# Cross attention in a perceiver layer on one core: scores computed once, their maxima reduced through 32 by 32 turns, elementwise work moved from VectorE

## The chip, the core and the metric

The kernel runs on one NeuronCore of a Trainium2 chip. TensorE (PE) multiplies matrices into PSUM, VectorE (DVE), ScalarE (ACT) and GpSimd (POOL) do the rest, SyncE (SP) issues transfers. The metric is the device time of one execution in microseconds (us), the median of several runs; lower is better. The profile is of one execution, and its spans and waits come from that one.

## The reference, cut to what matters

64 batch elements have 64 tokens of 256 features each, and each element has its own context of 256 tokens. One layer has three residual steps:

```python
x = x + xattn(layernorm(x), ctx, ctx)   # 16 heads of 16 features, keys and values from ctx
x = x + attn(layernorm(x))              # causal self attention, 16 heads
x = x + ffn(layernorm(x))               # silu(gate) * up, then down; inner width 1024
...
q = (queries @ Wq.T + bq).reshape(B, L, H, E)
k = (keys @ Wk.T + bk).reshape(B, S, H, E)
scores = jnp.einsum('blhe,bshe->bhls', q, k)
attn = jax.nn.softmax(scores * scale, axis=-1)
out = jnp.einsum('bhls,bshe->blhe', attn, v).reshape(B, L, H * E)
return out @ Wo.T + bo
```

In the FFN, activations are rounded to 8-bit integers with one scale per row (127 over the row's largest magnitude) and weights to -1, 0, 1 with one scale per matrix, ahead of each of the three products.

## The kernel before, in words

The elements are taken in nine groups (`GB`): seven of 8 and two of 4. Three stages of three groups run at the same time: cross attention of group g, self attention of group g-1, FFN of group g-2. Nothing is a loop over stages in program order. `layers` describes every step as an operation with an engine, an estimated cost, a due time `at` (one unit is about one batch element), and the buffers it reads and writes. `Graph.run` then plans: at each step it takes, over the engines, the operation that can start first, choosing on one engine by due time, by how much later it could start (`LATE`), and by whether ScalarE would have to load another function table (`TURN`); `AHEAD` bounds how far it may run in front of the oldest one left. `SHIFT` and `LAST` are per-kind offsets of the due times, `LAST` for those due after `END`, and `HURRY` and `SPURT` draw the last elements forward. The plan fixes the order on each engine; on the chip each engine goes through its list strictly in that order. Buffers come from rings with a few slots (`RINGS`). The score ring `sc` has one slot, [128, 4, 2, 256] f32, which is four of the eight PSUM banks; the other four banks are the ring `mm`, through which all other products pass.

Per pair of elements, `project` makes keys (line 484, evicted at 507) and values (519, evicted at 525). Per element, `cross` (line 587) does this:

1. `sc`, line 607: scores with queries on the partitions (two heads times 64 tokens), keys along the row, 4 head pairs at a time in four row groups of TensorE, twice.
2. `nm`, line 620: DVE takes the negated maximum of each row, 2048 elements to 8. `sc`'s slot is then free.
3. `terms`, lines 613 to 616: four small DVE steps split each maximum into three bf16 terms.
4. `mtp` (625) turns them on TensorE, and ACT copies them to `mT` (627).
5. `scT`: in the same kind of slot, the scores a second time, now with keys on the partitions. Line 638 first writes minus the maximum through a selecting matrix `sel` (bf16), line 643 adds the scores.
6. `exp`, line 648: two ACT steps of 1024 elements into `PT`, which frees the slot.
7. `av`, line 656: products with the values. The value tile carries ones, so that the same product gives the sums. Two heads share a product, and each half of the partitions has its numerators where the other has its sums.
8. `keep` (ACT, 672) scales one half by a 0/1 column, DVE merges it with the other half (677), shuffles the sums (678), takes their reciprocal (679), and POOL multiplies into `yT` (682).

Self attention uses the same `sc` slot for its scores `ssc` (line 725), twice per group; its hold ends when four mask additions on DVE (737) have read it. In the FFN, ACT normalises (459), DVE finds the row maxima (819) and multiplies each tile by its scale, adding a number that rounds (862); 512 columns at a time TensorE makes gate and up (882), ACT applies silu (889), and DVE multiplies up, its scale and silu (892) into `h`. Then come the row maximum, the rounding (ACT 908, DVE 911), a turn by transfer, and the product down (919).

`out_bias` (line 369) makes the two output bias rows once, near the start, from constants `brow` that were loaded over ACT's queue (1016).

Of the kernel before, what the change touches and what calls it, by code (L numbers as in the profile page):

```python
# [48 lines left out]
SC = S // P  # L50
GB = (8, 8, 8, 8, 8, 8, 8, 4, 4)
# [44 lines left out]
class Op:  # L96
# [15 lines left out]
STICK = 0.0005  # L112
TABLE = 1283.0
AHEAD = 5.691
HURRY, SPURT = 2.4886, 8
WAIT = 578031
LATE = 0.0129
TURN = 2.8858
# [6 lines left out]
    "ACT exp": -0.11, "ACT hqT f": -10.14, "ACT hscaled f": 1.99, "ACT k s": 0.18, "ACT keep": -0.9,  # L125
    "ACT mT": 1.22, "ACT norm a": 0.11, "ACT norm f": -2.03, "ACT norm s": 2.98, "ACT q s": -0.85,
    "ACT qT f": -11.74, "ACT sexp s": -0.59, "ACT silu f": -0.43, "ACT skeep s": 1.07, "ACT spT s": -3.21,
    "ACT turned a": -1.44, "ACT v a": -2.48, "ACT v s": -0.49, "DVE h f": 0.9, "DVE hq f": 0.13,
    "DVE hscales f": 1.37, "DVE mask s": 0.027, "DVE nm": 0.73, "DVE q f": 2.75, "DVE ratio": 0.51,
    "DVE rounded f": 3, "DVE smax s": 0.07, "DVE stats a": -2.45, "DVE stats f": -3.39, "DVE stot s": 0.805,  # L130
    "DVE wdown sums": 1.47, "DVE x a": -1.84, "DVE x f": 1.05, "DVE x s": 1.31, "PE av": -0.29,
    "PE down f": -0.64, "PE gate/up f": 0.1, "PE k a": 0.05, "PE mtp": 0.12, "PE q a": -0.24,
    "PE q s": 0.03, "PE sav s": -1.58, "PE sc": -0.38, "PE ssc": -0.13, "PE stp s": 0.21,
    "PE turn a": -0.11, "PE turn s": -1.7, "PE v a": -0.1, "PE v s": 2.11, "PE wgate total": 0.98,
    "POOL less s": -1.59, "POOL root a": 2.36, "SP load wgate": 1.56, "SP load wup": 1.17,
    "SP load x": -6.63,
# [3 lines left out]
    "ACT exp": -2.03, "ACT hqT f": 9.14, "ACT hscaled f": 1.51, "ACT keep": -0.53, "ACT mT": -2.79,  # L140
    "ACT norm s": -5.27, "ACT qT f": 9.17, "ACT sexp s": -1.13, "ACT silu f": 1.38, "ACT spT s": 2.36,
    "ACT v a": 3.26, "ACT v s": 1.58, "DVE h f": -0.28, "DVE hq f": 1.39, "DVE hscales f": 1.92,
    "DVE mask s": -1.27, "DVE nm": -2.37, "DVE q f": -2.35, "DVE ratio": 1.17, "DVE rounded f": -1.88,
    "DVE smax s": 0.59, "DVE stats f": 1.64, "DVE stats s": 2.35, "DVE stot s": -0.66, "DVE syT s": -0.92,
    "DVE x f": 2.71, "DVE x s": -2.93, "PE down f": 3.91, "PE gate/up f": 0.21, "PE hqtp f": 2.44,
    "PE k a": 3.27, "PE mtp": 1.86, "PE o s": -2.39, "PE sc": -0.79, "PE ssc": -1.18, "PE stp s": -0.27,
    "PE v a": -1.05, "PE v s": -1.66, "POOL less s": 2.66,
}
END = 59.061
# [177 lines left out]
def dve(n):  # L327
    return 65.0 + 1.044 * n
# [6 lines left out]
def layers(nc, a, out, R, c):  # L335
# [9 lines left out]
    msl = [Buf(t=c[f"msl_{i}"]) for i in range(2)]  # L345
# [23 lines left out]
    def out_bias(at, w, vcol, brow, res, name):  # L369

        rep = bufs("keep", [P, KC, P], f"rep_{name}")
# [4 lines left out]
        def product():  # L376
# [5 lines left out]
        op("DVE", dve(D), at, name, lambda: nc.vector.tensor_tensor(res.t, pm.t[:, 0:D], brow, ALU.add),  # L382
           reads=[pm], writes=[res])
# [203 lines left out]
    def cross(n, at):  # L587
# [5 lines left out]
        nm = bufs("nm", [P, NJ, KC], f"nm_{n}")  # L593
        ms = msl[n % 2]

# [6 lines left out]
        sc = bufs("sc", [P, NJ, KC, S], f"sc_{n}")  # L602

        def maxima():
            for hg in range(KC):
                for j in range(NJ):
                    nc.tensor.matmul(sc.t[:, j, hg, :], q(hg, j), kT.t[rows(j), hg, k0:k0 + S],  # L607
                                     start=True, stop=True)
# [373 lines left out]
def tile_perceiver(ctx: ExitStack, tc: tile.TileContext, a: dict, out: bass.AP):  # L982
# [32 lines left out]
    for i, name in enumerate(("bo_r", "bo2_r")):  # L1015
        nc.scalar.dma_start(c["brow"][:, i, :], a[name])
# [103 lines left out]
```

## Time and profile before

| | |
|---|---|
| median of 3 runs | 861.35 us (861.09 to 861.81) |
| profiled execution: its own time / its span | 862.48 us / 860.7 us |
| granted TensorE clock, mean | 0.99 |
| busy: PE / weight loads / DVE / ACT / POOL | 831.4 / 573.2 / 690.3 / 590.4 / 301.0 us |
| function table loads on ACT | 44 of 1.28 us |
| transfers | 41.8 MB, mean 49 GB/s |

The span is what the instructions cover in the profiled execution; that execution's own time is 1.8 us longer. Busy times are sums over an engine's instructions. In a group's row, the name of the written tile stands left of `<-` and those of the read ones right of it, then partitions x elements and type, then the count; after the first bar the busy time and the mean of one instruction, after the second the engine's idle time before them and what ended it. An f32 product appears as two matmul instructions. In the page's list of costliest groups the first two are the maxima over the scores (DVE, 144.7 us) and the exps (ACT, 125.1 us); the products of keys and of values follow with 122.7 and 122.6 us.

### The profile page before, as it was taken

The numbers are of one execution on the slowest core, as the hardware profiler recorded it, in microseconds if no ns is written. First come the engines' busy times: TensorE is split into PE (matmuls) and PEld (weight loads), VectorE is DVE, ScalarE is ACT, GpSimd is POOL, SyncE is SP. The second block draws the span as 40 slices with busy tenths as digits, with TensorE's granted clock in tenths as the row PEclk, the third lists the DMA queues.
The fourth block names the chain that finished last, engine by engine and source line by source line (L and its number), as shares of the span: only waits on it lengthen the run. The fifth ranks groups of instructions, "written<-read, shape, count | busy, mean of one in ns | idle before, by whom it ended". The sixth has DMA issues, their size and how long they took to land. (4 is left out here: it accounts for less than half of the span.)

```text
span 860.7 us, 28167 instructions
## 1 busy us (share of the span) xinstructions
PE 831.4 (97%) x12136; PEld 573.2 (67%) x12136; DVE 690.3 (80%) x1499; ACT 590.4 (69%) x948; POOL 301.0 (35%) x505
## 2 busy tenths in 40 slices
PE   8999899999999999999999999999999999998966
PEld 5766657776577756676667766777567775776633
DVE  2587678896888878988789886889779877999995
ACT  3554666547986597747886487865888487767855
POOL 3330527424242334405144152422344141354640
PEclk9999999999999999999999999999999999999988
DMA  7212201002022210222112111211012320011110
GB/s 264 76 51 100 75 27 51 27 3 62 14 51 64 57 40 6 51 88 39 38 38 51 39 39 39 50 58 51 8 39 51 64 38 14 14 27 39 26 37 38
DMA packets 47740, 41.82 MB, mean 49 GB/s; under 512 B 39168, under 2 KB 39680, under 8 KB 47616
## 3 DMA queue, kind: packets, MB, share of 16 engines
q1 hardware_dynamic: 45888, 39.59, 17.5%
q8 instruction: 95, 1.56, 0.7%
q10 hardware_dynamic: 1728, 0.43, 0.2%
q14 instruction: 29, 0.24, 0.1%
HBM read 26.65 MB, written 4.19 MB: 36 GB/s over the span
## 5 line engine op out<-in xcount | busy, mean ns | idle before, releaser
L620 DVE TENSOR_REDUCE nm<-sc 128x8 f32<-128x2048 f32 x64 | 144.7, 2261 | 27.9 <-PE sc L607 27.9
L648 ACT ACTIVATE PT<-scT 128x1024 f32<-128x1024 f32 x128 | 125.1, 1020 | 28.4 <-PE scT L643 28.1
L484 PE MATMUL k_a<-cT,wk 128*128 128x512 f32 x256 | 122.7, 609 | 2.5 <-DMA wk<-in_wk_dram 2.5
L519 PE MATMUL v_a<-wv,cT 128*128 128x256 f32 x512 | 122.6, 383 | 0.0
L682 POOL TENSOR_TENSOR yT_a<-keep 128x128 f32<-128x128 f32 x64 | 30.7, 480 | 247.7 <-DVE keep L679 189.0
L519 PEld LDWEIGHTS v_a<-wv,cT 128*128 128x128 f32 x512 | 95.0, 190 | 19.6 <-issue 3.2
L742 POOL TENSOR_TENSOR s_s<-s_s,smax_s 128x512 f32<-128x512 f32 (+1 forms) x72 | 67.3, 951 | 60.5 <-DVE smax_s L740 56.8
L507 ACT ACTIVATE kT<-k_a,bk_c 128x512 f32<-128x512 f32 x64 | 43.9, 685 | 59.4 <-PE k_a L484 59.1
L656 PEld LDWEIGHTS av<-PT,v 128*32 128x32 f32 x4096 | 60.4, 110 | 28.6 <-ACT PT L648 13.0
L484 PEld LDWEIGHTS k_a<-cT,wk 128*128 128x128 f32 x256 | 46.4, 192 | 47.5 <-issue 39.0
L752 POOL TENSOR_TENSOR s_s<-s_s,stot_s 128x512 f32<-128x512 f32 (+1 forms) x72 | 67.1, 952 | 27.6 <-DVE msl L613 12.3
L607 PE MATMUL sc<-kT,qm 32*128 32x256 f32 x1024 | 73.3, 400 | 3.0 <-ACT PT L648 3.0
L643 PE MATMUL scT<-qm,kT 32*128 32x128 f32 x2048 | 75.1, 270 | 0.0
L677 DVE SCALAR_TENSOR_TENSOR keep<-av,par,keep 128x256 f32<-128x256 f32 x64 | 30.6, 479 | 53.6 <-ACT keep L672 43.7
L656 PE MATMUL av<-PT,v 128*32 128x64 f32 x4096 | 71.4, 221 | 2.0 <-ACT PT L648 1.8
L643 PEld LDWEIGHTS scT<-qm,kT 32*128 32x128 f32 x2048 | 68.5, 186 | 0.2
L679 DVE RECIPROCAL keep<-keep 128x128 f32<-128x128 f32 x64 | 61.0, 953 | 2.2
L607 PEld LDWEIGHTS sc<-kT,qm 32*128 32x128 f32 x1024 | 46.2, 184 | 19.8 <-ACT PT L648 5.8
L737 DVE TENSOR_TENSOR s_s<-ssc,causal 128x512 f32<-128x512 f32 (+1 forms) x72 | 42.7, 620 | 13.4 <-PE ssc L725 13.2
L892 DVE SCALAR_TENSOR_TENSOR h_f<-up_f,units,silu_f 128x512 f32<-128x512 f32 x64 | 46.5, 739 | 7.7 <-ACT silu_f L889 6.3
L550 POOL TENSOR_TENSOR x<-x,bo_r 128x512 f32<-128x512 f32 x32 | 40.1, 1272 | 32.6 <-issue 16.7
L525 ACT COPY v<-v_a 128x512 f32<-128x512 f32 x64 | 37.2, 582 | 20.9 <-PE v_a L519 20.8
(156 smaller groups left out, 1677.6 us busy)
## 6 DMA issues: line engine op xcount, KB each, us to landing
cT<-in_ctx_dram SPq DMA_DIRECT2D x32, 512.0 KB, 3.4
x<-in_x_dram SPq DMA_DIRECT2D x7, 512.0 KB, 3.7
out_dram<-x SPq DMA_DIRECT2D x7, 512.0 KB, 2.8
wffn_gate<-in_wgate_dram SPq DMA_DIRECT2D x2, 512.0 KB, 5.8
wffn_up<-in_wup_dram SPq DMA_DIRECT2D x2, 512.0 KB, 5.7
wffn_down<-in_wdown_dram SPq DMA_DIRECT2D x2, 512.0 KB, 3.7
wqkv<-in_wqkv_dram SPq DMA_DIRECT2D x1, 768.0 KB, 7.4
x<-in_x_dram SPq DMA_DIRECT2D x2, 256.0 KB, 2.6
```

Of the source, the lines that this page charges most:

```text
L484: nc.tensor.matmul(pm.t[:, 0:n], w.t[:, kc, c0:c0 + P], src.t[:, kc, :], start=(kc == 0), stop=(kc == KC - 1))
L507: op("ACT", act(n) + 100, at, f"k {name}", lambda: nc.scalar.activation(kT.t[:, hg, :], pm.t[:, 0:n], AF.Identity, bias=bias), reads=[pm], ...
L519: nc.tensor.matmul(pm.t[:, i * D:(i + 1) * D], src.t[:, kc, (i0 + i) * P:(i0 + i + 1) * P], w.t[:, kc, c0:c0 + D], start=(kc == 0), stop=( ...
L607: nc.tensor.matmul(sc.t[:, j, hg, :], q(hg, j), kT.t[rows(j), hg, k0:k0 + S], start=True, stop=True)
L620: op("DVE", dve(NJ * KC * S), at, f"nm {n}", lambda: nc.vector.tensor_reduce(nm.t, sc.t, AX.X, ALU.max, negate=True), reads=[sc], writes=[nm])
L643: nc.tensor.matmul(sT.t[:, j, hg, s * P:(s + 1) * P], kT.t[rows(j), hg, k0 + s * P:k0 + (s + 1) * P], q(hg, j), start=False, stop=True, sk ...
L648: op("ACT", act(NJ * S), at + .03, f"exp {n}", lambda: nc.scalar.activation(pT.t[:, hg].rearrange("p j k n -> p j (k n)"), sT.t[:, :, hg, ...
L656: nc.tensor.matmul(av.t[rows(j), h, hg, :], v.t[:, ((n % 2) * SC + s) * NP + hg * NJ + j, 2 * h:2 * h + 2, :].rearrange("p a e -> p (a e)" ...
L679: nc.vector.reciprocal(t.t[:, 1], t.t[:, 1])
L742: op("POOL", pool(nt), p(k), f"less {nm}", lambda: nc.gpsimd.tensor_tensor(t.t, t.t, mx.t.unsqueeze(2).to_broadcast(full), ALU.subtract), ...
L752: op("POOL", pool(nt), p(k + 1), f"over {nm}", lambda: nc.gpsimd.tensor_tensor(t.t, t.t, tot.t.unsqueeze(2).to_broadcast(full), ALU.mult), ...
L892: op("DVE", dve(512) + 60, p(k), f"h {nm}", lambda: nc.vector.scalar_tensor_tensor(h.t[:, n0:n0 + 512], up.t, u.t[:, 1, i:i + 1], sl.t, AL ...
```

## The change

In `cross`, the scores are computed once, with keys on the partitions, as `scT`. DVE reduces them with `apply_transpose`: each 32 by 32 block is turned, and the maximum over its 32 keys is taken. That leaves, for each of the four partition quarters, the maxima over 32 keys. `larger` joins the two key halves and writes each result three times into `msl` (now f32); TensorE turns it (f32, 128 by 128); `terms`, now behind that turn and with four steps, takes the maximum over the quarters out of PSUM and makes the three bf16 terms straight into `mT`, each partition its own by means of per-partition factors `termpar`. `less` then subtracts the maximum by adding the `sel` product into the same PSUM tile, which has stayed in its slot, and the exps follow.

The merge of the two halves becomes a second ACT step `own` and a POOL addition `both`. In the FFN the first rounding goes from DVE to ACT, one step per tile; the gating becomes an ACT step (up times its scale, out of PSUM into `h`) and a POOL multiplication by silu. The bias rows are loaded over SP's queue into a slot of ring `h` when they are needed. New rings: `own` (1 slot), `less` (2); `nm` goes from 4 to 2. All planner numbers (`SHIFT`, `LAST`, `AHEAD`, `HURRY`, `LATE`, `TURN`, `STICK`, `WAIT`, `END`) are other ones, so the order on every engine differs.

```diff
...
-STICK = 0.0005
+STICK = 0
-AHEAD = 5.691
-HURRY, SPURT = 2.4886, 8
-WAIT = 578031
-LATE = 0.0129
-TURN = 2.8858
+AHEAD = 6.1849
+HURRY, SPURT = 3.4019, 8
+WAIT = 2308970000.0
+LATE = 0.0053
+TURN = 3.4322
...
+        row = bufs("h", [P, D], f"row_{name}")
+        op("SP", 60, at - 1, f"load {name}", lambda: nc.sync.dma_start(row.t, a[brow]), writes=[row],
+           size=D * 4 * P)
...
-        def maxima():
+        def scores():
+
             for hg in range(KC):
-                for j in range(NJ):
-                    nc.tensor.matmul(sc.t[:, j, hg, :], q(hg, j), kT.t[rows(j), hg, k0:k0 + S],
-                                     start=True, stop=True)
...
                 for s in range(SC):
                     for j in range(NJ):
                         nc.tensor.matmul(sT.t[:, j, hg, s * P:(s + 1) * P],
                                          kT.t[rows(j), hg, k0 + s * P:k0 + (s + 1) * P], q(hg, j),
-                                         start=False, stop=True, skip_group_check=True)
+                                         start=(hg == s == 0), stop=False,
+                                         skip_group_check=True)
...
+        op("DVE", dve(NJ * KC * S), at, f"nm {n}", lambda: nc.vector.tensor_reduce(
+            nm.t.rearrange("p a s b -> p (a s b)"),
+            sT.t.rearrange("p j c (b q) -> p (j c b) q", q=32), AX.X, ALU.max, apply_transpose=True),
+           reads=[sT], writes=[nm])
+
+        op("DVE", 230, at + .01, f"larger {n}", lambda: nc.vector.tensor_tensor(
+            ms.t, nm.t[:, :, 0, :].unsqueeze(3).to_broadcast([P, NJ * KC, QB, 3]),
+            nm.t[:, :, 1, :].unsqueeze(3).to_broadcast([P, NJ * KC, QB, 3]), ALU.max),
+           reads=[nm], writes=[ms])
+        pt = tile_of(f"mtp_{n}")
+        mT = bufs("mT", [P, QB, 32], f"mT_{n}", BF16)
+        op("PE", 110, at + .02, f"mtp {n}", lambda: nc.tensor.transpose(
+            pt.t[:, 0:P], c[f"msl_{n % 2}"].rearrange("p a s -> p (a s)"), c["ident"]), reads=[ms],
+           writes=[pt], holds=[mT])
...
+            y, z = less.t[:, 0], less.t[:, 1]
+            upper = lambda t: t.bitcast(BF16)[:, 1::2]
+            stt = nc.vector.scalar_tensor_tensor
+            nc.vector.tensor_reduce(y, pt.t[:, 0:P].rearrange("p (g q) -> p q g", q=32), AX.X, ALU.max,
+                                    negate=True)
+            stt(z, upper(y), c["termpar"][:, 0:1], y, ALU.mult, ALU.add)
+            stt(y, upper(z), c["termpar"][:, 1:2], z, ALU.mult, ALU.add)
+            stt(mT.t, upper(y).unsqueeze(1).to_broadcast([P, QB, 32]), 1.0,
+                c["termpar"][:, 2:2 + QB].unsqueeze(2).to_broadcast([P, QB, 32]), ALU.mult, ALU.mult)
...
+        def without():
+            for hg in range(KC):
+                for j in range(NJ):
+                    nc.tensor.matmul(sT.t[:, j, hg, :], c["sel"][rows(j), hg, :],
+                                     mT.t[rows(j)].rearrange("p b q -> p (b q)").unsqueeze(1).to_broadcast(
+                                         [2 * E, SC, P]), start=False, stop=True, skip_group_check=True)
...
+        op("PE", KC * pe(S, BF16) + 40, at + .03, f"less {n}", without, reads=[mT], writes=[sT], mode="rows",
+           holds=[pT])
...
+        op("ACT", act(2 * KC * T) + 100, at + .05, f"own {n}", lambda: nc.scalar.activation(
+            u.t.rearrange("p h c q -> p (h c q)"), av.t.rearrange("p h c q -> p (h c q)"),
+            AF.Copy, scale=c["par"][:, 0:1]), reads=[av], writes=[u])
+        op("POOL", pool(2 * KC * T) + 100, at + .055, f"both {n}", lambda: nc.gpsimd.tensor_tensor(
+            t.t, t.t, u.t, ALU.add), reads=[u], writes=[t])
...
-            nc.vector.scalar_tensor_tensor(t.t, av.t, c["par"][:, 0:1], t.t, ALU.mult, ALU.add)
...
-        def rounded():
-            for i in range(ni):
-                nc.vector.tensor_scalar(xn.t[:, i, :], xn.t[:, i, :], scale.t[:, i:i + 1], MAGIC,
-                                        ALU.mult, ALU.add)
+        def rounded(i):
+            op("ACT", act(D) + 215, p(2.2), f"rounded {nm}", lambda: nc.scalar.activation(
+                xn.t[:, i, :], xn.t[:, i, :], AF.Identity, scale=scale.t[:, i:i + 1], bias=c["magic"]),
+               reads=[scale], writes=[(xn, i)])
...
-            op("DVE", dve(512) + 60, p(k), f"h {nm}", lambda: nc.vector.scalar_tensor_tensor(
-                h.t[:, n0:n0 + 512], up.t, u.t[:, 1, i:i + 1], sl.t, ALU.mult, ALU.mult),
-               reads=[up, u, sl], writes=[(h, n0)])
+            op("ACT", act(512) + 100, p(k), f"up {nm}", lambda: nc.scalar.activation(
+                h.t[:, n0:n0 + 512], up.t, AF.Copy, scale=u.t[:, 1, i:i + 1]), reads=[up, u],
+               writes=[(h, n0)])
+            op("POOL", pool(512), p(k), f"h {nm}", lambda: nc.gpsimd.tensor_tensor(
+                h.t[:, n0:n0 + 512], h.t[:, n0:n0 + 512], sl.t, ALU.mult), reads=[sl], writes=[(h, n0)])
...
```

## The prediction, made before the changed kernel ran

> **What bounds it now.** I read the busy row of the page first, then PE by stretches of the span, then what PE waited for, then the costliest groups, then single instructions in order of time.
>
> The page's busy row, and three stretches of one group of eight batch elements each (columns: length, busy us of each engine, granted clock, DMA share, GB/s):
>
> ```profile
> PE 831.4 (97%) x12136; PEld 573.2 (67%) x12136; DVE 690.3 (80%) x1499; ACT 590.4 (69%) x948; POOL 301.0 (35%) x505
> ```
> ```profile
> 228.00:329.00 101.00, 100.99 (x1510) 69.66 (x1507) 84.81 (x181) 73.30 (x116) 34.31 (x57) 1.00 0.20 46
> 329.00:430.00 101.00, 101.00 (x1524) 69.92 (x1520) 83.72 (x180) 73.38 (x115) 33.86 (x56) 1.00 0.20 46
> ...
> 790.00:861.00 71.00, 53.69 (x470) 32.03 (x469) 59.64 (x150) 47.32 (x84) 25.09 (x59) 0.90 0.14 38
> ```
>
> In the middle PE has no gap at all, and every other engine has room; only the last 71 us (the last groups' self attention and FFN, a chain) leave it idle. [...]
>
> ```profile
> 424.07 1.15 PE L607 MATMUL sc<-kT,qm 32*128 32x256 f32 x16
> 425.15 1.98 PE L484 MATMUL k_s<-xnT_s,wqkv 128*128 128x512 f32 x4
> ```
>
> The next product starts 1.08 us after the first `sc` matmul. An `sc` step really keeps PE for 1.08 us, back to back; I go by the row. PE's waits are small too:
>
> ```profile
> PE qtp_f L836 <- DVE q_f L869: 4.4, 2, 4.2
> PE sc L607 <- ACT PT L648: 3.0, 4, 1.5
> ```
>
> The groups that the sum uses (busy us, mean ns of one | idle before, releaser):
>
> ```profile
> L620 DVE TENSOR_REDUCE nm<-sc 128x8 f32<-128x2048 f32 x64 | 144.7, 2261 | 27.9 <-PE sc L607 27.9
> L648 ACT ACTIVATE PT<-scT 128x1024 f32<-128x1024 f32 x128 | 125.1, 1020 | 28.4 <-PE scT L643 28.1
> ...
> L752 POOL TENSOR_TENSOR s_s<-s_s,stot_s 128x512 f32<-128x512 f32 (+1 forms) x72 | 67.1, 952 | 27.6 <-DVE msl L613 12.3 <-DVE stot_s L749 8.8 <-ACT keep L672 3.1
> ...
> L892 DVE SCALAR_TENSOR_TENSOR h_f<-up_f,units,silu_f 128x512 f32<-128x512 f32 x64 | 46.5, 739 | 7.7 <-ACT silu_f L889 6.3 <-PE up_f L882 1.1
> ...
> L677 DVE SCALAR_TENSOR_TENSOR keep<-av,par,keep 128x256 f32<-128x256 f32 x64 | 30.6, 479 | 53.6 <-ACT keep L672 43.7 <-POOL rstd_a L449 4.7 <-ACT v L525 2.7
> L672 ACT ACTIVATE keep<-av,par 128x256 f32<-128x256 f32 x64 | 30.6, 479 | 23.1 <-PE av L656 22.0 <-ACT spT_s L765 0.6 <-DVE stot_s L749 0.4
> ```
>
> **The part-by-part sum.** PE, per batch element (64 of them). Gone: the `sc` step, 1.08. The turned scores with their subtraction take 1.22 now (starts 419.90 to 421.12); in that, each of two `sel` quadruples holds 0.11. Split, they make about 1.00 + 0.22 and the same number of row-group steps (two before, two after), so I add 0 to 0.1 for a second pipe fill and take 0.03. The maxima are turned in f32 in place of bf16: f32 transposes start about 0.11 apart (`stp`), bf16 ones about 0.06 (`hqtp`), so +0.05. Net -1.00, 64 us in all; one group of eight, which repeats every 100.8 us (its `ssc` starts at 328.51, 429.24, 530.05), would be PE-bound at 92.8.
>
> DVE. Gone: L677 30.6, L892 46.5, and the FFN rounding at L862 9.4 us, 86.5 together. The four small maxima steps (0.20 to 0.24 each, 0.84) become `larger` (96 elements; 512 cost 0.62 and 8 cost 0.2, so about 0.3) and four `terms` (32 to 128 elements, 0.2 to 0.3, 0.95): +0.41, 26 us. The transposing reduce has no row. Its nearest is L620: the same 2048 f32 from the same PSUM tile, 2.26 us. [...] Bounds: no less than 2.2 (the same elements must be read), no more than 4.5 (two passes). I take 2.26, the row; 4.5 is a rival. DVE goes from 690 to 630.
>
> ACT: the `mT` copy goes (17.2); `own` comes, 64 x 0.479 as L672 (30.6); the up product's scaling, 64 x about 0.66 (silu of 512 takes 0.687, a copy of 512 0.582), 42; the rounding, 32 x 0.59 as `xn_f`, 19. 590 becomes 665. POOL: `both`, 256 elements, between 0.48 (128 elements, `yT`) and 0.95 (512), 0.64 x 64 = 41; `h`, 512 elements, 0.952 x 64 = 61; 301 becomes 403. [...] The rows say 0.952 against 0.739, 61 us. [...] I book +2. The rings `own` (one slot) and `keep` (two) are held some 1.5 us longer through `both`; at over 10 us from one element to the next that is nothing. The two bias rows now come over SP's queue (128 KB each) instead of ACT's; whatever loads are queued behind them there are put back by under 3.4 us each, which is what a load four times as large takes to land, and they fall within the first 25 us, where PE is busy 21.6 of 25: 0, at worst 2.
>
> **The new wait.** The score tile `sc` takes four PSUM banks and has one slot. From the timeline I took every hold of it: first maxima product to end of reduce, mean 4.31 us (least 3.50); turned scores to end of second exp, mean 3.78 (least 3.30); self attention's `ssc` to its fourth mask, mean 5.27, two per group; and 1.26 mean between holds. Now the slot is free while the maxima are made into terms, turned and copied, and two elements alternate in it. After the change one element holds it from scores to exp. Least hold: scores 1.0, hop 0.2, reduce 2.26, `larger` 0.3, hop 0.3, transpose 0.23, hop 0.25, terms 0.95, hop 0.3, `less` 0.3, hop 0.2, two exps 1.94; that is 8.2, and 0.2 to the next start: 8.4. (Hops from the trace: 0.33 from DVE's end to a PE load, 0.2 from PE to ACT or DVE.) A group then needs 8 x (8.4 + w) + 2 x 6.2 us, w being the queueing per element at its six engine entries: PE three times, DVE twice, ACT once. Two waits are in-order stops: PE's transpose and `less` have projections, FFN products and `av` queued behind them; `terms` on DVE has masks, sums and the next statistics behind it. If they come early, all those stand.
>
> w from both sides: 0.3 if the order always fits (group 81, PE binds at 92.8). As high as 3.8 if each entry waits as now: 0.81 (DVE) and 0.48 (ACT) above the least, 0.96 (PE) before a start, about 0.5 for each of the three other entries. That makes a group 110. Today's waits arise where nothing hurried; a PE product of 1.7 us cannot be interrupted, though, and PE is full of them. I take the middle, 1.9: 8 x 10.3 + 12.4 = 94.8 us, 2.0 above PE's own bound. So of 64 us on PE, 16 go to the slot.
>
> Sum on the profiled execution (span 860.7, its time 862.48, so 1.8 around the span): 860.7 - 8 x 6.0 = 812.7, + 2 for the tail, + 1.8 = 816.5; the runs' median is 1.1 below that execution, so 815.
>
> **Rivals.** 1. PE still binds and the slot just fits (w at most 1.65): 862.5 - 64 + 2 - 1 = 799. For it: PE was gapless, and the least hold leaves room. Against: six entries in a row, three at a full PE. 2. The slot binds and the kernel is slower. It decides from a hold plus gap of (100.8 - 12.4)/8 = 11.05 us per element, w = 2.65; at w = 3.3 a group takes 106 and the kernel 903. For it: the present means above; and an order fixed ahead turns each late maximum into a stop of PE. Against: PE and DVE then have more room, and the waits shrink themselves. 3. The transposing reduce runs at half rate: +2.2 us in each hold, about 112 per group, near 950; DVE at 770 does not bind, the slot does. [...]
>
> **Numbers.** Main case, part of the gain lost to the slot (w 1.65 to 2.5, 800 to 850): 0.44, 815. Rival 1: 0.24. Rival 2: 0.18. Rival 3: 0.10. Rival 4: 0.04. A measurement tells about 0.2% of 861, 1.7 us, from no change; so faster 0.68, same 0.04, slower 0.28. The range goes from 792 (rival 1 with a shorter tail) to 895 (rival 2 in most of its width), leaving out rival 3 and the edges. The faster cases alone span 792 to 850.
>
> **What would show it.** No `sc` product and `scT` starts 1.00 apart from what follows; the reduce at 2.2 to 2.4 us; the group's period (between `ssc` starts) near 95; the slot's hold near 9.5 with a mean gap under 1; PE near 97% of a shorter span, or 90% with waits at `mtp` and `less` in case 2. POOL near 400, ACT near 665, DVE near 630. The prediction is wrong if the reduce takes over 3 us, if holds average over 10.5 us, or if ACT's table loads (44 now, 1.28 us each) multiply and stand before exps.

## The result and the profile after

The changed kernel takes 892.42 us (median of 4 runs, 889.85 to 894.54) against 861.58 us of the kernel before beside it: ratio 1.036, 95% interval 1.0325 to 1.039. It is slower by about 31 us; the forecast was 815. The profiled execution, the fastest of the four, has a span of 887.8 us.

The busy row of the page after:

```profile
PE 806.7 (91%) x11112; PEld 537.6 (61%) x11112; DVE 681.5 (77%) x1403; ACT 655.1 (74%) x1046; POOL 428.5 (48%) x633
```

The second product is gone (11,112 matmuls in place of 12,136), yet PE's busy time falls by 24.7 us and not by 64. VectorE was to fall by 60 us and falls by 9.

Where the time came from is seen when the span is cut at the first `ssc` product of the first group and at that of the seventh. Between the two cuts lie six whole group periods. They hold the scores and exps of 47 elements before and of 48 after, for the first stretch passes 12 elements before and 11 after. Stretches of the kernel before, then of the kernel after (length, busy us of PE, weight loads, DVE, ACT, POOL, granted clock, DMA share, GB/s):

```profile
0.00:135.30 135.30, 128.27 (x1769) 86.54 (x1769) 88.13 (x186) 72.09 (x118) 43.11 (x67) 0.99 0.28 94
135.30:724.20 588.90, 586.28 (x8837) 406.65 (x8830) 480.51 (x1023) 424.06 (x667) 202.73 (x332) 1.00 0.18 43
724.20:860.70 136.50, 116.86 (x1538) 79.96 (x1537) 121.66 (x291) 94.22 (x163) 55.20 (x107) 0.95 0.12 29
```
```profile
0.00:135.70 135.70, 116.85 (x1379) 74.18 (x1379) 84.34 (x165) 66.70 (x107) 52.62 (x76) 0.95 0.28 94
135.70:732.50 596.80, 566.14 (x8126) 378.54 (x8126) 476.75 (x965) 468.33 (x736) 283.70 (x418) 0.99 0.17 42
732.50:887.80 155.30, 123.72 (x1612) 84.89 (x1611) 120.41 (x273) 120.03 (x205) 92.20 (x140) 0.90 0.11 27
```

Six groups went from 588.9 to 596.8 us, the last stretch from 136.5 to 155.3, the first stayed. In the middle PE had no gap before and now stands still for 5.1 us of each group (596.8 - 566.1, over six). In the last stretch PE is busy *longer* than before, 123.7 us against 116.9, though a product was removed; the granted clock there is 0.90 against 0.95.

What PE waits for in the kernel after (us in total, times, longest), and the groups of the new chain and of GpSimd:

```profile
PE scT L660 <- DVE mT L649: 28.4, 30, 2.0
PE mtp L634 <- DVE msl L628: 6.6, 10, 2.0
```
```profile
L623 DVE TRANSPOSE_TENSOR_REDUCE nm<-scT 128x64 f32<-128x2048 f32 x64 | 147.6, 2307 | 56.6 <-PE scT L614 56.2
...
L918 POOL TENSOR_TENSOR h_f<-h_f,silu_f 128x512 f32<-128x512 f32 x64 | 81.6, 1285 | 55.3 <-ACT silu_f L912 34.3 <-ACT h_f L915 20.9
...
L696 POOL TENSOR_TENSOR keep<-keep,own 128x256 f32<-128x256 f32 x64 | 47.3, 739 | 91.8 <-ACT own L693 91.5
```
```profile
L648 DVE SCALAR_TENSOR_TENSOR less<-less,termpar 128x32 f32<-128x32 bf16 x64 | 29.2, 457 | 2.3
L647 DVE SCALAR_TENSOR_TENSOR less<-less,termpar 128x32 f32<-128x32 bf16 x64 | 27.6, 432 | 2.3
L649 DVE SCALAR_TENSOR_TENSOR mT<-less,termpar 128x128 bf16<-128x128 bf16 x64 | 26.4, 412 | 2.2
L628 DVE TENSOR_TENSOR msl<-nm 128x96 f32<-128x96 f32 x64 | 24.8, 387 | 2.1
...
L645 DVE TENSOR_REDUCE less<-mtp 128x32 f32<-128x128 f32 x64 | 16.8, 263 | 12.9 <-PE mtp L634 12.6
```

The largest wait stands at `less`, for the last step of `terms`: the new wait that the prediction named. The transposing reduce is as quick as the row it was costed by, 2.31 against 2.26 us. The small steps behind it are not: the four that read two operands take 387 to 457 ns in the mean, while their medians are 252 to 292 and single ones reach 1.33 us. Single instructions in order of time show what happens (start, us, engine and line):

```profile
409.89 0.25 DVE L648 SCALAR_TENSOR_TENSOR less<-less,termpar 128x32 f32<-128x32 bf16 x1
...
420.35 1.26 POOL L557 TENSOR_TENSOR x<-x,bo_r 128x512 f32<-128x512 f32 x1
420.47 1.19 DVE L648 SCALAR_TENSOR_TENSOR less<-less,termpar 128x32 f32<-128x32 bf16 x1
...
421.70 0.29 DVE L649 SCALAR_TENSOR_TENSOR mT<-less,termpar 128x128 bf16<-128x128 bf16 x1
...
422.04 0.40 PE L660 MATMUL scT<-mT,sel 32*128 32x256 bf16 x8 [1.42 <-DVE mT L649]
```

The same step of 32 elements takes 0.25 us with GpSimd idle and 1.19 us when a GpSimd addition of two SBUF operands has begun just before; both end within 0.05 us of each other, and PE stands for 1.42 us behind it. Over the whole trace the steps that start while GpSimd works take 0.53 us (L628), 0.56 (L647), 0.75 (L648) and 0.94 (L649), the others 0.25 to 0.31. `nm` and the first step of `terms` (L645) read PSUM and are not stretched: those that start while GpSimd works take 2.30 and 0.26 us, the others 2.32 and 0.26. Added up, the four steps take 41 us more than undisturbed. Put down to the GpSimd instruction that overlaps each most, 16 us of this stand beside the two new steps (L696, L918) and 25 beside steps that the kernel before had too (12 at L774, 9 at L557).

### The profile page after: what moved, and what is told of

Same layout as the page of the kernel before. It is cut to its first block, busy times and chain, and to the rows that moved or that the text cites. A ratio compares the mean times of both kernels' runs of the same rounds, so it can differ in the third digit from the quotient of the medians.

```text
span 887.8 us, 26233 instructions
## 1 busy us (share of the span) xinstructions
PE 806.7 (91%) x11112; PEld 537.6 (61%) x11112; DVE 681.5 (77%) x1403; ACT 655.1 (74%) x1046; POOL 428.5 (48%) x633
## 4 chain that ended last, share of the span: by engine, by line
PE 45%; DVE 37%; ACT 9%; POOL 3%; issue 3%; DMA 3%; ACTq 0%; SPq 0%; POOLq 0%; DVEq 0%
DVE nm L623 8%; PE k_a L491 8%; PE scT L614 5%; PE v_a L526 5%; DVE s_s L759 3%; DVE smax_s L762 3%; PE q_a L491 3%; ACT PT L665 3%; PE av L673 3%; DVE stot_s L770 3%; DVE less L648 3%; PE k_s L491 3%; PE down_f L944 2%; DVE less L647 2%; DVE keep L701 2%
## 5 line engine op out<-in xcount | busy, mean ns | idle before, releaser
L623 DVE TRANSPOSE_TENSOR_REDUCE nm<-scT 128x64 f32<-128x2048 f32 x64 | 147.6, 2307 | 56.6 <-PE scT L614 56.2
L491 PE MATMUL k_a<-cT,wk 128*128 128x512 f32 x256 | 126.0, 620 | 0.7 <-DMA wk<-in_wk_dram 0.7
L918 POOL TENSOR_TENSOR h_f<-h_f,silu_f 128x512 f32<-128x512 f32 x64 | 81.6, 1285 | 55.3 <-ACT silu_f L912 34.3
L696 POOL TENSOR_TENSOR keep<-keep,own 128x256 f32<-128x256 f32 x64 | 47.3, 739 | 91.8 <-ACT own L693 91.5
L774 POOL TENSOR_TENSOR s_s<-s_s,stot_s 128x512 f32<-128x512 f32 (+1 forms) x72 | 67.8, 955 | 34.6 <-DVE stot_s L771 34.0
L614 PEld LDWEIGHTS scT<-qm,kT 32*128 32x128 f32 x2048 | 64.5, 190 | 28.6 <-issue 15.2
L759 DVE TENSOR_TENSOR s_s<-ssc,causal 128x512 f32<-128x512 f32 (+1 forms) x72 | 40.7, 619 | 20.5 <-PE ssc L747 20.5
L660 PE MATMUL scT<-mT,sel 32*128 32x256 bf16 x512 | 25.9, 276 | 28.6 <-DVE mT L649 28.4
L690 ACT ACTIVATE keep<-av,par 128x256 f32<-128x256 f32 x64 | 30.2, 472 | 27.4 <-PE av L673 27.4
L841 DVE TENSOR_REDUCE amax_hf<-h_f 128x1 f32<-128x1024 f32 x32 | 38.4, 1201 | 12.7 <-POOL h_f L918 12.6
```

Of the source, the lines that this page charges most:

```text
L491: nc.tensor.matmul(pm.t[:, 0:n], w.t[:, kc, c0:c0 + P], src.t[:, kc, :], start=(kc == 0), stop=(kc == KC - 1))
L614: nc.tensor.matmul(sT.t[:, j, hg, s * P:(s + 1) * P], kT.t[rows(j), hg, k0 + s * P:k0 + (s + 1) * P], q(hg, j), start=(hg == s == 0), stop ...
L623: op("DVE", dve(NJ * KC * S), at, f"nm {n}", lambda: nc.vector.tensor_reduce(nm.t.rearrange("p a s b -> p (a s b)"), sT.t.rearrange("p j c ...
L696: op("POOL", pool(2 * KC * T) + 100, at + .055, f"both {n}", lambda: nc.gpsimd.tensor_tensor(t.t, t.t, u.t, ALU.add), reads=[u], writes=[t])
L759: op("DVE", dve(nt), p(k), f"mask {nm}", lambda: nc.vector.tensor_tensor(t.t, sc.t[:, j, 0:nt].rearrange("p (b k) -> p b k", k=T), c["caus ...
L774: op("POOL", pool(nt), p(k + 1), f"over {nm}", lambda: nc.gpsimd.tensor_tensor(t.t, t.t, tot.t.unsqueeze(2).to_broadcast(full), ALU.mult), ...
```

## The theories

**A.** The one score slot sets the pace. Its hold is longer than was reckoned because `larger` and three steps of `terms` are stretched beside GpSimd, to which the change gives more work.

**B.** Something else costs the time, and the slot only follows: the early bias rows, the longer gating chain at the end, the mere order of the new plan, or the offloads.

Every hold of the slot was read from the timeline, from the first score product to the end of the second exp, with the gap to the next start (of any user of the slot). "Six groups" is the mean of the six periods above, "end" the stretch behind them.

| kernel | median us | ratio to before (95%) | span | hold + gap | six groups, each | end |
|---|---|---|---|---|---|---|
| before | 861.6 | | 860.7 | two holds, 4.31 and 3.78; 1.26 | 98.2 | 136.5 |
| after | 892.4 | 1.036 (1.0325 to 1.039) | 887.8 | 9.85 + 1.07 | 99.5 | 155.3 |
| e1 one SBUF operand | 853.4 | 0.989 (0.987 to 0.992) | 848.9 | 9.38 + 0.97 | 95.1 | 146.7 |
| e2 two terms steps | 853.3 | 0.990 (0.989 to 0.992) | 850.6 | 9.40 + 0.98 | 95.4 | 147.5 |
| e3 thin GpSimd | 873.0 | 1.013 (1.011 to 1.015) | 870.7 | 9.69 + 1.06 | 97.7 | 148.0 |
| e6 later bias rows | 887.0 | 1.029 (1.027 to 1.032) | 888.4 | 9.94 + 1.10 | 99.5 | 155.6 |
| e11 gating back at the end | 896.2 | 1.038 (1.036 to 1.040) | 889.7 | 9.85 + 1.05 | 99.3 | 157.2 |
| e7 short steps, new order | 853.5 | 0.990 (0.989 to 0.992) | 851.4 | 9.18 + 1.11 | 95.2 | 154.2 |
| e15 the same, other order | 854.4 | 0.992 (0.990 to 0.993) | 850.8 | 9.36 + 1.13 | 96.1 | 147.2 |
| e8 as e7, no offloads | 893.0 | 1.036 (1.034 to 1.037) | 890.7 | 9.88 + 1.33 | 97.4 | 155.4 |
| e10 scores once, no offloads | 913.7 | 1.061 (1.056 to 1.066) | 907.6 | 10.69 + 0.85 | 100.3 | 162.9 |
| e13 offloads alone | 897.2 | 1.042 (1.040 to 1.045) | 894.2 | two holds, 4.06 and 3.97; 1.40 | 101.9 | 144.3 |
| e14 short steps, same order | 847.0 | 0.983 (0.981 to 0.984) | 845.9 | 9.34 + 0.95 | 94.6 | 146.9 |
| e16 as e14, half the keys product | 837.9 | 0.972 (0.970 to 0.974) | 833.3 | 9.31 + 0.83 | 93.7 | 144.9 |

## The experiments

In e1, e2, e3, e11, e14 and e16 the planner's costs and offsets are those of the change, so that (but for e11's few last slices) every engine keeps its order. In e7, e8, e10, e13 and e15 the offsets are new.

### e1: the same steps, one operand each from PSUM

```diff
-            nm.t[:, :, 1, :].unsqueeze(3).to_broadcast([P, NJ * KC, QB, 3]), ALU.max),
+            sT.t.rearrange("p j c (b q) -> p (j c) b q", q=64)[:, :, :, 0:3], ALU.max),
...
-            stt(z, upper(y), c["termpar"][:, 0:1], y, ALU.mult, ALU.add)
-            stt(y, upper(z), c["termpar"][:, 1:2], z, ALU.mult, ALU.add)
+            stt(z, upper(y), c["termpar"][:, 0:1], pt.t[:, 0:32], ALU.mult, ALU.min)
+            stt(z, upper(z), c["termpar"][:, 1:2], pt.t[:, 0:32], ALU.mult, ALU.min)
-            stt(mT.t, upper(y).unsqueeze(1).to_broadcast([P, QB, 32]), 1.0,
-                c["termpar"][:, 2:2 + QB].unsqueeze(2).to_broadcast([P, QB, 32]), ALU.mult, ALU.mult)
+            stt(mT.t, upper(y).unsqueeze(1).to_broadcast([P, QB, 32]), 1.0 / 12.0,
+                pt.t[:, 0:P].rearrange("p (b q) -> p b q", q=32), ALU.mult, ALU.min)
```

> Same plan and order on every engine, same number and size of steps; the four small VectorE steps inside the score slot's hold (larger, and three of the four terms) take their second operand from PSUM instead of SBUF. Leaves out the right subtraction (other numbers are subtracted from the scores). Theory A (the one score slot binds, and these steps are stretched from 0.25-0.29 to 0.5-0.9 us whenever GpSimd is reading SBUF): they fall to their least, 0.67 us less hold per element, 64 x 0.67 = 43 us, of which about 30 reach the end: 862. Rival B (the gating and merging moved to ScalarE and GpSimd set the time): no change, 889 to 893. Rival C (the loss is in the start and the tail of the plan): 885 to 892.

Measured: 853.38 us. The four groups of steps that took two SBUF operands:

```profile
L649 DVE SCALAR_TENSOR_TENSOR mT<-less,mtp 128x128 bf16<-128x128 bf16 x64 | 17.9, 280 | 0.0
...
L628 DVE TENSOR_TENSOR msl<-nm,scT 128x96 f32<-128x96 f32 x64 | 16.1, 252 | 2.1
L648 DVE SCALAR_TENSOR_TENSOR less<-less,termpar,mtp 128x32 f32<-128x32 bf16 x64 | 15.9, 248 | 2.3
L647 DVE SCALAR_TENSOR_TENSOR less<-less,termpar,mtp 128x32 f32<-128x32 bf16 x64 | 15.9, 248 | 2.3
```

All four stand within 0.02 us of the least that they take in the change (0.29, 0.25, 0.25 and 0.25 us); the longest of `larger` is 0.26 us and of the whole `terms` 1.06, with GpSimd as busy as in the change (427.6 us). PE's wait at `less` falls from 28.4 us to 4.4:

```profile
PE scT L660 <- DVE mT L649: 4.4, 9, 1.1
```

The stretches:

```profile
0.00:131.70 131.70, 117.05 (x1382) 75.18 (x1383) 79.66 (x165) 66.45 (x107) 52.59 (x76) 0.95 0.30 96
131.70:702.20 570.50, 556.14 (x8095) 375.24 (x8124) 445.33 (x965) 466.41 (x735) 282.20 (x418) 1.00 0.18 43
702.20:848.90 146.70, 118.28 (x1602) 81.90 (x1611) 114.17 (x273) 118.85 (x206) 92.76 (x141) 0.93 0.12 29
```

With the number of steps, their order and the work of the other engines unchanged, 38.9 us of span are gone: 26.3 in the six groups, 8.6 at the end, 4.0 at the start. Hold and gap fell from 10.92 to 10.35; 64 times 0.57 is 36.5. Without the stretch the kernel is 1.1% below the one before in place of 3.6% above it. One thing more differs in e1. The last step of `terms` no longer needs what the step ahead of it wrote, and starts 0.08 us before that one ends, where in the change it starts 0.03 us after. So 0.12 of the 0.78 us by which `larger` and `terms` get shorter is not stretch. With this share taken off, an estimate of 33 of the 38.9 us remains, still more than the 27.1 us by which the change's span exceeds that of the kernel before.

In the rows here L647 takes 432 ns in the mean with two SBUF operands and 248 with one, both times beside a busy GpSimd (428.5 and 427.6 us); L645, whose one operand is in PSUM, takes 263 in the change and 264 in e1.

### e2: two steps of `terms` in place of four

```diff
-            stt(z, upper(y), c["termpar"][:, 0:1], y, ALU.mult, ALU.add)
-            stt(y, upper(z), c["termpar"][:, 1:2], z, ALU.mult, ALU.add)
-            stt(mT.t, upper(y).unsqueeze(1).to_broadcast([P, QB, 32]), 1.0,
+            stt(mT.t, y.unsqueeze(1).to_broadcast([P, QB, 32]), 1.0,
...
```

`termpar` keeps one of the three copies of each maximum, in a line that is left out here.

> Same plan and order; two of the four terms steps are left out, so one bf16 number per maximum is subtracted instead of a sum of three (softmax does not change by what is subtracted). Theory A: the hold falls by two steps of 0.43 and 0.46 us and their 0.03 us gaps, 0.95 us per element, 61 us, of which about 35 reach the end (then TensorE's work is next): 857. Rival B: no change, since neither ScalarE nor GpSimd does less: 889 to 893. Rival C: at most 5 us.

Measured: 853.32 us. `terms` takes 0.79 us in place of 1.67; the hold falls as in e1, to 9.40, and so does the time. What leaves the chain inside the slot comes off the time, whether it was stretch or steps, but not in full. Of the 0.88 us, 0.42 come back as a longer way from the end of `mT` to the start of `less` (0.69 us for 0.27; in e1 it is 0.55).

### e3: the same chain, GpSimd's new work made thin

```diff
-            t.t, t.t, u.t, ALU.add), reads=[u], writes=[t])
+            t.t[:, 1], t.t[:, 1], u.t[:, 1], ALU.add), reads=[u], writes=[t])
...
-                h.t[:, n0:n0 + 512], h.t[:, n0:n0 + 512], sl.t, ALU.mult), reads=[sl], writes=[(h, n0)])
+                h.t[:, n0:n0 + 16], h.t[:, n0:n0 + 16], sl.t[:, 0:16], ALU.mult), reads=[sl], writes=[(h, n0)])
```

> Same plan and order; GpSimd's two new steps are cut: the gating multiplies 16 of 512 columns, the merge adds only the half with the sums. Leaves out most of the gating and half of the merge. GpSimd falls from 428 to about 335 us. Theory A: the gain comes only through less stretching of the terms (these two steps stand beside some 14 us of the 43 us of stretch) and a few us at the end of the last chain: 872 to 882. Rival B: GpSimd's work and its latency are the cause, so most of the 31 us come back: 860 to 868. Rival C: only the tail, 880 to 885.

Measured: 872.95 us, in A's range. GpSimd is busy 344.9 us in place of 428.5, and the steps that were not touched get shorter:

```profile
L647 DVE SCALAR_TENSOR_TENSOR less<-less,termpar 128x32 f32<-128x32 bf16 x64 | 28.7, 448 | 2.3
L649 DVE SCALAR_TENSOR_TENSOR mT<-less,termpar 128x128 bf16<-128x128 bf16 x64 | 25.0, 391 | 2.2
L648 DVE SCALAR_TENSOR_TENSOR less<-less,termpar 128x32 f32<-128x32 bf16 x64 | 21.9, 343 | 2.3
...
L628 DVE TENSOR_TENSOR msl<-nm 128x96 f32<-128x96 f32 x64 | 20.8, 325 | 2.1
```

L648 falls from 457 to 343 ns, L628 from 387 to 325, L647 hardly moves. A little under half of what e1 recovers comes back, 17 us of span. Not all of that is stretch: the four steps lose 12 us of their 41, and the way from the slot's last release to the end is 4 us shorter (48.0 for 52.2). The 29 us of stretch that remain stand for the most part beside GpSimd's old steps (L774 and L557, 22 us), which the kernel before had too.

### e6: the bias rows where the planner would put them

```diff
-    "ACT turned s": -0.14, "ACT up f": 1.2, "ACT v a": -0.19, "ACT v s": 1.1, "DVE bo r": -6.72,
+    "ACT turned s": -0.14, "ACT up f": 1.2, "ACT v a": -0.19, "ACT v s": 1.1,
...
-    "PE av": 1.72, "PE bo r": -2.99, "PE down f": 0.54, "PE k s": -0.72, "PE mtp": -0.83, "PE o a": -0.97,
+    "PE av": 1.72, "PE down f": 0.54, "PE k s": -0.72, "PE mtp": -0.83, "PE o a": -0.97,
```

> The two due-time offsets that drew the bias rows' steps to the very front are taken out, so VectorE and TensorE take the first statistics and keys before them; the order differs only within the first 45 products. Theory C: the first score product starts at 24 to 25 us instead of 30.6, and all 6 us are carried to the end: 886. Theory A: the same, as the slot is full from its first use on, a later first use is a later end: 886; it does not tell these two apart but sizes the start's part of the loss. If the start is hidden by later slack: 892.

Measured: 886.96 us, between the two values. The slot is used 7.4 us earlier (23.3 for 30.6 us), but the first `ssc` stays at 136.0 us and so do the groups and the end; the profiled span, 888.4, is not shorter at all. The profile of e6 is of its slowest execution, though, and that of the change of its fastest; the medians are 5.5 us apart, and their intervals do not overlap (1.027 to 1.032, 1.0325 to 1.039). So up to 5 us of the early delay may show in the time, in a place that these two traces do not tell.

### e11: the gating of the last two groups back on VectorE

```diff
+            if g >= NG - TURNS:
+                op("DVE", dve(512) + 60, p(k), f"h {nm}", lambda: nc.vector.scalar_tensor_tensor(
+                    h.t[:, n0:n0 + 512], up.t, u.t[:, 1, i:i + 1], sl.t, ALU.mult, ALU.mult),
+                   reads=[up, u, sl], writes=[(h, n0)])
+                return
```

> The changed kernel, with the feed-forward gating of the last two groups (of four sequences each) back on VectorE in one step; all else as in the change, offsets too. Theory A (the end is 9 to 10 us longer than before because in the last chain each slice of 512 goes through ScalarE's extra copy, 0.7 us, and a GpSimd product of 1.28 us in place of one VectorE step of about 0.65 us, with nothing left to hide it): 884 to 889 us, and the stretch from the last release of the score slot to the end falls from 52 to 44 to 48 us. Rival B (the end is longer because the groups reach it later and TensorE's granted clock is lower there, not because of the gating): 891 to 894 us, the last stretch still 50 to 53 us.

Measured: 896.21 us, not faster; the end is 157.2 us, of which 54.7 follow the slot's last release, against 52.2 in the change. The longer gating chain is not what lengthens the end: Theory A of this run falls.

### e14 and e16: what sets the pace once the stretch is gone

e14 takes both costs away at once; `mT` and its selecting factors `termpar` then hold one term:

```diff
-        op("DVE", 230, at + .01, f"larger {n}", lambda: nc.vector.tensor_tensor(
-            ms.t, nm.t[:, :, 0, :].unsqueeze(3).to_broadcast([P, NJ * KC, QB, 3]),
-            nm.t[:, :, 1, :].unsqueeze(3).to_broadcast([P, NJ * KC, QB, 3]), ALU.max),
+        op("DVE", 230, at + .01, f"larger {n}", lambda: nc.vector.tensor_reduce(
+            ms.t[:, :, :, 0], nm.t.rearrange("p a s b -> p a b s"), AX.X, ALU.max),
...
-            y, z = less.t[:, 0], less.t[:, 1]
+            y = pt.t[:, P:P + 32]
...
-            stt(mT.t, upper(y).unsqueeze(1).to_broadcast([P, QB, 32]), 1.0,
-                c["termpar"][:, 2:2 + QB].unsqueeze(2).to_broadcast([P, QB, 32]), ALU.mult, ALU.mult)
+            nc.vector.tensor_tensor(mT.t, y.unsqueeze(1).to_broadcast([P, QB, 32]),
+                                    c["termpar"][:, 2:2 + QB].unsqueeze(2).to_broadcast([P, QB, 32]), ALU.mult)
...
```

> The changed kernel in its own order (planner costs and offsets untouched), with larger as one reduction that reads one operand, and with terms as two steps, the maximum and one product that reads one operand from PSUM: the maximum is kept as one bf16 value in place of three. Both known costs of the hold are then gone at once, the stretch beside GpSimd and two of the steps. Theory A (the slot's hold sets the pace, so that time falls by some 64 us for each us of hold): hold 8.7 to 9.0 against 9.4 in each of the two kernels that took away one cost alone, 825 to 842 us. Rival B (with hold and gap at 10.3 the slot has already stopped setting the pace: TensorE, whose idle time was down to 2.4 us per group there, and the last stretch bind): 846 to 854 us, the hold shorter but the gap between holds longer, groups still 94 to 96 us apart.

Measured: 846.97 us, the fastest kernel here that computes the whole layer, 1.7% below the kernel before. It falls in B's range, but the hold did not get shorter, as B had it. The chain on VectorE is 0.46 us shorter than in e1 (0.22 + 0.60 for 0.25 + 1.03), yet the hold is the same, 9.34: the time from the end of `mT` to the start of `less` grew from 0.55 to 0.92 us. In that interval PE is not idle (1.1 us of 58.8 in sum over all elements); it works through other products, projections above all, that the plan, which still expects 0.9 us of `terms`, put in front of `less`. Whether PE then binds, as B says, is tried by leaving out half of the keys' product (PE's busy time falls by 48 us, 58 were expected):

```diff
-            for kc in range(KC):
+            half = 1 if name.startswith("k_a") else KC
+            for kc in range(half):
...
```

> The kernel with short steps in the change's own order, with half of the product that makes cross attention's keys left out (one of its two feature chunks, so the keys are not the right ones; some 58 us of TensorE's time are gone, 7.3 us of each group); everything else and the order as they were. Theory A (once the stretch is gone the slot no longer sets the pace and TensorE does): most of the 58 us comes off, less what the slot then holds back: the mean hold plus gap falls from 10.3 to 9.5 to 9.8, groups come 88 to 91 us apart, 800 to 822 us. Rival B (the slot's chain of six stops still sets the pace at 10.3 us, whatever TensorE has to do): 838 to 847 us, TensorE idle for 8 to 10 us of each group.

Measured: 837.85 us. Middle stretch of e14, then of e16:

```profile
131.30:699.00 567.70, 555.19 (x8096) 374.58 (x8125) 428.14 (x869) 466.62 (x735) 281.75 (x418) 1.00 0.18 44
```
```profile
126.20:688.40 562.20, 523.76 (x7997) 358.17 (x8026) 428.19 (x869) 465.93 (x735) 282.69 (x418) 0.99 0.18 44
```

PE loses 31.4 us of work in the six groups and they get 5.5 us shorter; PE now stands idle for 6.4 us of each, no other engine is above 83%, and hold and gap go only from 10.28 to 10.14. (Each of the two traces lacks 29 matmul records of the six groups, which can make the idle time too large by up to 0.8 us per group.) The time lies at the lower edge of B's range. So PE's amount of work was not what held the kernel at 847 us, against A of this run. What remains is the chain of six stops in a fixed order, as B says; that the order is the part to change is argued, not shown.

### e7, e15, e8, e10, e13: the parts, each with an order of its own

e7 is the change with the short steps of e14, `"DVE bo r"` and `"PE bo r"` dropped, the planner told the measured costs, and new offsets; e15 has other offsets again:

```diff
-        op("DVE", dve(NJ * KC * S), at, f"nm {n}", lambda: nc.vector.tensor_reduce(
+        op("DVE", 2310, at, f"nm {n}", lambda: nc.vector.tensor_reduce(
...
-        op("DVE", 200 + 2 * 200 + 300, at + .02, f"terms {n}", terms, reads=[pt], writes=[less, mT])
+        op("DVE", 620, at + .02, f"terms {n}", terms, reads=[pt], writes=[pt, mT])
...
-            op("POOL", pool(512), p(k), f"h {nm}", lambda: nc.gpsimd.tensor_tensor(
+            op("POOL", 1285, p(k), f"h {nm}", lambda: nc.gpsimd.tensor_tensor(
```

> The whole change with a shorter chain in the slot's hold: larger is a reduction with one input, terms is two steps (maximum over the quarters written to PSUM, one masked product), one bf16 number per maximum; the planner is given the measured costs and its offsets are searched anew. Theory A: hold near 8.7 us and a hold plus gap of 9.5, 64 x 9.5 + 18 x 5.8 = 712, with 75 for start and tail 787; TensorE's own work of about 800 then binds together with it: 835 to 845. Rival B (ScalarE's and GpSimd's new work sets the time): not under 860, as that work is untouched. Rival C (start and tail): 850 or more.

> The kernel with short steps, planner costs as measured and offsets searched anew, after a search of the offsets four times as long, which ends at a plan 3.5 us shorter (830.6 against 834.1). If the plan's gain comes through: 847 to 851 us against 853.5 of the first search. If the last stretch, where the run loses 10 us to the plan, eats it: 852 to 857 us.

Measured: 853.51 and 854.44 us. Both miss the better ends of what was expected: e7 was to reach 835 to 845, and e15's plan, 3.5 us shorter, came to nothing. A new order with right costs is not better than the change's own order with short steps (e14). Told apart are only causes of tens of us, not of five.

e8 and e10 keep the scores computed once and give gating, merge and rounding back to VectorE, e8 with short steps and e10 with all four; e13 is the kernel before with the offloads alone. Each undoes the corresponding part of the diff.

> As e7_short_replanned, but gating, merging and the first rounding are back on VectorE (offsets searched anew, same effort). Theory A: VectorE has 86 us more and the hold enters it twice, so its queueing grows, hold plus gap near 10.3: 860 to 868. Rival B (those moves to ScalarE and GpSimd are what costs): faster than e7_short_replanned, 830.

> The other half alone: scores once, with the four terms as in the change; gating, merging and rounding on VectorE (offsets searched anew, same effort). Theory A: the long hold is there and VectorE is fuller, so the slot binds harder than in the whole change: 888 to 905. Rival B: without the moves the saved products show: 820 to 850.

> The kernel before with the offloads alone (gating product, merge of the two halves and rounding leave VectorE, bias rows are loaded as in the change), scores still computed twice, planner costs as measured and offsets searched anew. Theory A (before, TensorE and the slot set the pace, not VectorE; relief of VectorE pays only once the slot hold depends on how fast VectorE answers): 858 to 872 us, VectorE's busy time 60 to 75 us below the kernel before. Rival B (the offloads are worth by themselves what they were worth in the changed kernel with short steps, some 20 to 40 us): 822 to 842 us.

Measured: 892.96, 913.73 and 897.16 us, each slower than either of its theories expected. The offloads are worth 39 us where the scores are computed once (e8 against e7) and cost 35 where they are computed twice (e13). Scores computed once without the offloads are the slowest of all, with VectorE at 747.5 us and a hold of 10.69. In these orders neither half pays by itself, and both together do, once the chain is short. A caution: the orders are not those of the change, and how much of each loss is order is open; the PE of e13 is busy at least 10.7 us more than before with the same products.

Taken together, A is shown, for about 33 of the 39 us that e1 gives back. Of B, the early bias rows cost at most some 5 us (e6), the gating at the end nothing (e11), and the order is the same in e1; part of the longer end is explained by neither.

## Why the prediction was wrong

**What bounded the kernel before: right.** PE stood still for 0.4 us per group, and the kernel with the offloads alone (e13, in an order of its own) gained nothing.

**PE's saving: a fifth too large.** `scT` takes 1.10 from start to start (taken: 1.00), `less` 0.33 (0.22), `mtp` 0.14 (0.12): together 1.57 against 2.37 before, 0.80 per element and not 1.00, 51 us and not 64. The 0.03 us added for a second pipe fill was the author's estimate, and no run shows it as such; what they show is that, split in two, each part takes 0.1 us more than was booked. The error does not enter the 815, which the slot set. PE's busy time fell by another 26 us less, 24.7 in all, since products that were not touched took longer (`k_a` 126.0 us for 122.7, `stp_s` 40.6 for 36.3), at a mean granted clock of 0.969 for 0.990.

**The reduce: right.** 2.31 for 2.26 us; the rival of half rate falls.

**The small steps: the step that failed first.** "`larger` [...] about 0.3" and "four `terms` [...] 0.95" make 1.25 us in each hold; they took 0.39 and 1.67, together 2.06. Undisturbed, `terms` takes 1.16 us in the change, so 0.2 of the difference is size and the rest is time beside GpSimd, a term that the sum does not have. e1, with 0.25 and 1.03, is 0.78 us shorter in each hold, of which 0.57 reach the pace, and with it 39 us of the 73 us between the forecast's span, 814.7, and 887.8 (33 without the other difference that e1 has). VectorE's busy time tells the same: forecast 630, 681.5 in the change, 639.2 in e1. The kernel before had shown it. Its four steps of 8 elements take 0.15 to 0.17 us when GpSimd is idle and 0.36 to 0.42 when it works, and the prediction used their means as if they were plain durations. One of them, then one of the new ones (ns, least/median/longest):

```profile
L614 DVE SCALAR_TENSOR_TENSOR nm<-msl,nm x64: 166/168/1187, 27.7 to 776.3; 128x8 f32<-128x8 bf16 x64
```
```profile
L648 DVE SCALAR_TENSOR_TENSOR less<-less,termpar x64: 250/252/1192, 36.2 to 797.7; 128x32 f32<-128x32 bf16 x64
```

**GpSimd's new work: booked too low.** POOL ended at 428 us where the sum had 403, `h` at 1.29 us and `both` at 0.74 where 0.95 and 0.64 were taken; the 64 products for `h` made 82 us, not 61. In the 815 there are only 2 us for the tail beside this work. No run shows that term: the end took 155.3 us for 136.5 before, and with the gating of the last two groups back on VectorE (e11) it took 157.2. The two steps' work costs 17 us by e3, for the larger part on VectorE, inside the slot. The mean of L752 was also the wrong row for `h`: it mixes two shapes, and one of its operands is broadcast. In the kernel before, its two shapes and the step with two full operands (L550) are:

```profile
L752 POOL TENSOR_TENSOR s_s<-s_s,stot_s 128x512 f32<-128x512 f32 x56 | 57.4, 1044 | 22.4 <-DVE msl L613 12.3 <-DVE stot_s L749 8.4 <-ACT s_s L744 1.2
L752 POOL TENSOR_TENSOR s_s<-s_s,stot_s 128x256 f32<-128x256 f32 x16 | 9.7, 630 | 5.2 <-ACT keep L672 3.1 <-ACT s_s L744 1.1 <-ACT skeep L790 0.7
L550 POOL TENSOR_TENSOR x<-x,bo_r 128x512 f32<-128x512 f32 x32 | 40.1, 1272 | 32.6 <-issue 16.7 <-ACT xn_s L459 15.7
```

**Queueing and hold: right, in part by luck.** With the stretch gone, hold and gap are 10.35 us (e1), forecast 10.3, and a group 95.1, forecast 94.8. The shortest hold in e1 is 7.83 us (8.2 forecast), the mean 9.38, so that queueing does add to each hold. That it came to 1.9 us was the middle taken between 0.3 and 3.8.

**The sum over the span: the second step that failed.** "860.7 - 8 x 6.0" took the period of a middle group, 100.8, for all of them and spread its gain over the whole span. The six periods average 98.2, so that 94.8 gains 3.4 each, and the first and last stretch gain nothing: in e1 they are 131.7 and 146.7 us, together 6.6 more than before, where 12 less plus 2 were booked. That makes the other 34 us, between 814.7 and the 848.9 of e1: 18 in the six groups and 17 at the two ends. In the first stretch the slot is full as well: from its first use on, it is held for 94% of the time in e1 and in the change, and it passes 11 elements there for 12 before. By the same slip the decision point of rival 2 was set at 11.05; with 98.2 it is (98.2 - 12.4) / 8 = 10.7, and 10.92 lies beyond it. So rival 2 is what came, at a smaller hold than its 903 us supposed.

**The start: mis-sized, mostly hidden.** The prediction gave the bias rows 2 us at worst for their transfers. The two loads took 6.1 us to land (5.4 before), where under 3.4 was taken, and two VectorE copies drawn to the front with them waited 5.4 us for another constant (`bv_c`), so that the first statistics came 8 us later (14.4 for 6.4 us). Of that at most some 5 us reach the time (e6).

**What stays open** is part of the end: 155.3 us, and still 146.7 in e1, against 136.5. Of the 18.8 us, 9 lie before the last group's first `ssc` starts (93.0 us from the seventh group's, 84.0 before); five elements still pass the slot there, and e1 takes 7.6 of the 9 away. The other 10 lie behind it. From the slot's last release to the end it is 52.2 us, 41.9 before, and neither the short steps (51.2 in e1, 51.9 in e14) nor the gating (e11) move that; e3 takes 4 us off. In the other orders it is 41.5 (e8) to 54.2 us (e15). What makes these 10 us is not shown.

## What to carry to other kernels

Where a buffer with one slot is held across several engines, each small step in it is paid once per turn, here by half to three quarters of its length (0.57 of 0.78 us in e1, 0.54 of 0.88 in e2, in hold and gap): sum hold and gap with the durations that the steps have beside the other engines' work, and look at the spread of a row, not only its mean. That GpSimd has room does not make work given to it free: VectorE steps with two SBUF operands paid for it here (L647: 432 ns in the mean), and an operand left in PSUM took them out of its way (248 in e1). And a gain per period holds only for the periods that are bound as the one it was read from; the first and the last stretch need a sum of their own.

## What the runs showed of the hardware

A VectorE step of 32 elements can take 1.19 us in place of 0.25 beside one GpSimd instruction, and the pair ends together, within 0.05 us (L648 and L557 in the change, at 420 us). A 32 by 32 transposing maximum over 2,048 f32 elements in PSUM costs as much as the plain one, 2.31 against 2.26 us. A GpSimd product of 512 f32 takes 1.28 us with two full operands, 1.04 with one of them broadcast. With the same products, PE's busy sum was 796 us in one order (e7, granted clock 0.976), 807 in another (the change, 0.969) and 812 in a third (e8, 0.960); f32 products of 512 columns in `k_a` took 609 ns in the mean before and 620 in the change, where PE stands still for 5.1 us of each group in place of 0.4; the cause is not shown.
